# One condition row spread by TensorE, one root for four tiles of x, and slot 0 with high and low weights in turn

## The chip, the core and the metric

The kernel runs on one core of a Trainium2 chip. The core has TensorE (PE: matmuls and transposes, with PEld for its weight loads), VectorE (DVE), ScalarE (ACT), GpSimd (POOL) and SyncE (SP), and 16 DMA engines that all issuing engines share. Each engine works through its own instructions in order; PE's matmuls write PSUM, which DVE and ACT read. The metric is the device time of one launch in microseconds, the median over the runs.

## The reference

A gated MLP layer on x of shape (4, 1024, 512), float32, with a condition per batch element:

```python
scale = cond @ norm_w.T + 1.0                     # (4, 512)
ms = mean(x * x, axis=-1)
h = x * (scale[:, None, :] * rsqrt(ms + 1e-6))
val, gate = split(h @ up_w.T, 2, axis=-1)         # up_w: (4096, 512)
h = val * gelu(gate)                              # 2048 wide
y = act_quant(h) @ weight_quant(down_w).T         # 8-bit tokens, ternary weights
return y + x
```

cond is (4, 128), norm_w (512, 128), down_w (512, 2048).

## The kernel before

The four batch elements are worked one after the other, 1024 tokens each, in two halves of 512. The up projection of a batch element has 16 blocks `j` of 128 value rows and 128 gate rows. Its products are fp16 with a split: each float32 operand is a high part and a low part, and a product is high*high + high*low + low*high. From batch 1 on, a block is one call of `slot`, with seven sub-products in place of eight (line 470). In batch 0, where up_w still has to be read, scaled, transposed and split, the products are the plain ones (line 485), and block 0 of the first half has a function of its own, `plain_first` (line 527). Everything is issued in an order written out by hand (`tc.manual_schedule()`), so the order in the text is the order on every engine's queue.

The change touches the start, up to the first matmuls of block 1. Its steps, in the names of the code:

- `cond_load(0, 1)` brings the first row of cond to all 128 partitions (64 KB) on ACT's queue, then norm_w (`nw`) follows. The other three rows come by `cond_load(1, B)` much later.
- `first_load(n)` brings tiles n and n+1 of x (128 tokens x 512, 512 KB together), `w_load(j)` block j of up_w (two of 256 KB, gate `t=1` and value `t=0`), all on SP's queue.
- `keep_warm(n)` issues n matmuls on zeros (line 752).
- `cond_scale` (line 160) is four dot products on DVE; `cond_largest`, `cond_over` (a transpose on PE, line 185), `cond_range` (four small DVE operations) and `cond_spread` (a matmul, line 201) bring the largest scale, rounded down to a power of two, to all partitions; `cond_undo` and `cond_bring_first` divide by it into `scT`.
- `first_sum(n)` squares tile n and sums (ACT, line 712); `rsqrt_start` takes the root of the sums (one ACT square root at 719, five small DVE operations, 720 to 724), for two tiles at a time; `first_scale` multiplies the tile (ACT 729 or DVE 731); `first_turn` transposes it on PE (line 736) into four banks `ptx`.
- `first_high(0, k)` writes the high part of `XP` from bank k (ACT, line 740), `first_low` the low part (DVE, line 744).
- `w_range`, `w_scale`, `w_turn`, `w_high`, `w_low` find the power-of-two range of a weight block, scale it, transpose it on PE (line 273) and write its high parts (ACT, 286 to 289) and low parts (DVE, 295 to 298). `w_evac` (line 302) copies the transposed block out for later sums.
- `plain_first` has two hooks: `second_part` (turn and split the value of block 0, remaining low parts of x, `w_evac(0)`, and the load of the Gelu table, line 813) and `second_slot` (turn and split block 1). After it comes `plain_half(1, 0)`, whose first matmul reuses the bank that block 0's Gelu (line 532) has to read first.

The bank tags "A", "B", "E" and "po" are PSUM banks; R and H are two large SBUF tiles that many views share.

Of the kernel before, what the change touches and what calls it, by code (L numbers as in the profile page):

```python
# [8 lines left out]
F32 = mybir.dt.float32  # L9
# [4 lines left out]
ALU = mybir.AluOpType  # L14
# [3 lines left out]
P = 128  # L18
# [23 lines left out]
def glu_quant_kernel(  # L42
# [10 lines left out]
    PE, ACT, DVE, POOL, SP = nc.tensor, nc.scalar, nc.vector, nc.gpsimd, nc.sync  # L53
    B, S, D = x.shape
    C = cond.shape[1]
    FF = down_w.shape[1]
    TOK = 512
    HALF = D // 2
    NA = TOK // P
    NK = D // P  # L60
# [6 lines left out]
    sm = ctx.enter_context(tc.tile_pool(name="small", bufs=2))  # L67
# [8 lines left out]
    ones = one.to_broadcast([P, P])  # L76
# [8 lines left out]
    H = cpool.tile([P, NSLOT, 2, TOK], F32, name="H")  # L85
# [10 lines left out]
    for n in range(0, P, 32):  # L96
        c = slice(n, n + 32)
# [18 lines left out]
    XP = R[:, 0, 0:4096].bitcast(F16)  # L116
    XP = XP.rearrange("p (l k t) -> p l k t", l=2, k=NK)
# [20 lines left out]
    def bank(tag, bufs, shape=None, name=None):  # L138
        return psum.tile(shape or [P, TOK], F32, name=name or tag, tag=tag, bufs=bufs)

    def po_bank(name, shape=None):
        return bank("po", 3, shape, name)


    scT = cpool.tile([P, NK, B], F32, name="scT")
    dx = cpool.tile([P, B], F32, name="dx")
    ux = cpool.tile([P, B], F32, name="ux")
    nw = R[:, 1, 0:512].rearrange("p (k c) -> p k c", k=NK)
    cb = R[:, 1, 512:1024].rearrange("p (b c) -> p b c", b=B)
    dots = R[:, 1, 1024 : 1024 + C]  # L150
    junk = R[:, 1, 2048:4096].rearrange("p (n d) -> p n d", d=D)

    def cond_load(b0, b1):

        v = cond[b0:b1].rearrange("b c -> (b c)").partition_broadcast(P)
        ACT.dma_start(out=cb[:, b0:b1].rearrange("p b c -> p (b c)"), in_=v)

    def cond_scale(b):
        for k in range(NK):
            DVE.scalar_tensor_tensor(  # L160
                dots, nw[:, k], 1.0, cb[:, b], ALU.mult, ALU.mult, accum_out=scT[:, k, b : b + 1]
            )

    def cond_scale_rest():
# [23 lines left out]
    def cond_range(pm, b0, b1):  # L188
        n = b1 - b0
        d4 = sm.tile([B, 1], F32, name=f"d4_{b0}", tag="d4")[:n]  # L190
        DVE.tensor_reduce(d4, pm, AX.X, ALU.max)
        DVE.tensor_scalar(d4, d4, 1e-30, None, ALU.max)
        pow2_floor(d4)
        dg = sm.tile([B, B], F32, name=f"dg_{b0}", tag="dg")[:n, :n]
        DVE.tensor_scalar(dg, ident[:n, :n], d4, 1.0 / X_UP, ALU.mult, ALU.mult)
        return dg

    def cond_spread(dg, b0, b1, tag):
        n = b1 - b0
        pd = bank(tag, {"po": 3}.get(tag, 2), [P, B], f"pd_{b0}")[:, :n]  # L200
        PE.matmul(pd, ones[:n, :], dg, start=True, stop=True)
        return pd

    def cond_undo(pd, b0, b1):
        DVE.tensor_copy(dx[:, b0:b1], pd)
        DVE.reciprocal(ux[:, b0:b1], dx[:, b0:b1])
# [35 lines left out]
    def w_load(j, ts=(1, 0)):  # L242
        for t in ts:
            SP.dma_start(out=wn(j)[:, t], in_=up_v[j][:, t])

    def w_range(j, t0=0, t1=2):
        t = slice(t0, t1)
        am = sm.tile([P, 2], F32, name=f"wam_{j}_{t0}", tag="wam")[:, t]
        DVE.tensor_reduce(am, wn(j)[:, t], AX.X, ALU.max, apply_absolute_value=True)
        pow2_floor(am)  # L250
        DVE.tensor_scalar(sw[:, j, t], am, 2.0**-100, 1.0 / W_UP, ALU.max, ALU.mult)
        if j not in iv:
            iv[j] = sm.tile([P, 2], F32, name=f"iv_{j}", tag="iv", bufs=3)
        DVE.reciprocal(iv[j][:, t], sw[:, j, t])
# [4 lines left out]
    def w_scale(j, ts=(1, 0), eng=POOL):  # L259
        for t in ts:  # L260
            w, r = wn(j)[:, t], iv[j][:, t : t + 1]
            if eng is ACT:
                ACT.activation(w, w, AF.Copy, scale=r)
            else:
                eng.tensor_scalar(w, w, r, 1.0, ALU.mult, ALU.mult)
# [25 lines left out]
    def w_low(j, ts=(1, 0)):  # L291
        gate, a21, a22 = a_parts(j)
        g, v = (p.rearrange("p (n f) -> p n f", n=2) for p in pw[j])
        if 1 in ts:
            DVE.tensor_tensor(gate[:, :, 1], g, gate[:, :, 0], ALU.subtract)
        if 0 in ts:
            DVE.tensor_tensor(a21[:, 1], v[:, 0], a21[:, 0], ALU.subtract)
            DVE.tensor_tensor(a22[:, 1], v[:, 1], a22[:, 0], ALU.subtract)
# [216 lines left out]
    def plain_first(between):  # L515

        ps = {1: bank("B", 1, name="pg_0_0"), 0: bank("A", 2, name="pv_0_0")}
        gate, a21, a22 = a_parts(0)
        for n, (t, w, l) in enumerate(
            ((1, 0, 0), (1, 1, 0), (0, 0, 0), (0, 1, 0), (1, 0, 1), (0, 0, 1))  # L520
        ):
            if n in between:
                between[n]()
            a = [gate[:, 0], gate[:, 1]] if t else [a21, a22]
            a = [v.rearrange("p w (k f) -> p w k f", k=2) for v in a]
            for k in range(NK):
                PE.matmul(
                    ps[t], a[k // 2][:, w, k % 2, :], XP[:, l, k, :TOK],
                    start=w + l + k == 0, stop=l == 1 and k == NK - 1,
                )  # L530
        t1 = wpool.tile([P, TOK], F32, name="g_0_0", tag="t1")
        ACT.activation(t1, ps[1], AF.Gelu, scale=gain(0, 1))  # L532
        DVE.scalar_tensor_tensor(h_half(0, 0), ps[0], gain(0, 0), t1, ALU.mult, ALU.mult)
# [156 lines left out]
    start_t = sm.tile([P, 1], F32, name="start_t", bufs=1)  # L690
    eps = sm.tile([P, 1], F32, name="eps", bufs=1)
    DVE.memset(eps, EPS)
    cond_load(0, 1)
    ACT.dma_start(out=nw, in_=norm_w.rearrange("(k p) c -> p k c", p=P))
    ACT.activation(start_t, one, AF.Sqrt)

# [9 lines left out]
    ssq0 = sm.tile([P, 8], F32, name="ssq0", bufs=1)  # L706
    rs0 = sm.tile([P, 8], F32, name="rs0", bufs=1)

    def first_sum(n, eng=ACT):
        v, j, a = X0[:, n], junk[:, n % 4], ssq0[:, n : n + 1]  # L710
        if eng is ACT:
            ACT.activation(j, v, AF.Square, accum_out=a)
        else:
            eng.scalar_tensor_tensor(j, v, 1.0, v, ALU.mult, ALU.mult, accum_out=a)

    def rsqrt_start(t, y):

        z = sm.tile([P, 2], F32, name="newton", tag="newton")
        ACT.activation(z, t, AF.Sqrt, scale=1.0 / D, bias=eps)
        DVE.tensor_scalar(t, t, 1.0 / D, EPS, ALU.mult, ALU.add)  # L720
        DVE.reciprocal(y, z)
        DVE.tensor_tensor(z, y, y, ALU.mult)
        DVE.scalar_tensor_tensor(z, z, -0.5, t, ALU.mult, ALU.mult)
        DVE.scalar_tensor_tensor(y, z, 1.5, y, ALU.add, ALU.mult)

    def first_scale(n, eng):
        r = rs0[:, n : n + 1]
        if eng is ACT:
            ACT.activation(X0[:, n], X0[:, n], AF.Copy, scale=r)
        else:  # L730
            eng.tensor_scalar(X0[:, n], X0[:, n], r, 1.0, ALU.mult, ALU.mult)

    def first_turn(n, pts):
        for k in range(NK):
            c = (n % NA) * P
            PE.transpose(pts[k][:, c : c + P], X0[:, n, k * P : (k + 1) * P], ident)  # L736

    def first_high(h, k, pt):
        c = slice(h * TOK, (h + 1) * TOK)
        ACT.activation(XP[:, 0, k, c], pt, AF.Copy, scale=scT[:, k, 0:1])  # L740
# [7 lines left out]
    def keep_warm(n):  # L748

        pz = bank("A", 2, name="pz")  # L750
        for i in range(n):
            PE.matmul(pz, warm[:, :P], warm, start=True, stop=True)

    first_load(0)
    w_load(0, (1,))
    first_load(2)
    w_load(0, (0,))
    w_load(1)
    first_load(4)
    first_load(6)  # L760
    w_load(2)
    keep_warm(18)
    first_sum(0)
    first_sum(1)
    cond_scale(0)
    mx = cond_largest(0, 1)
    pm = cond_over(mx, 0, 1, "A")
    rsqrt_start(ssq0[:, 0:2], rs0[:, 0:2])
    first_scale(0, ACT)
    first_scale(1, ACT)  # L770
    keep_warm(4)
    pd = cond_spread(cond_range(pm, 0, 1), 0, 1, "A")
    first_sum(2)
    first_sum(3)
    w_range(0, 1, 2)
    w_scale(0, (1,), DVE)
    cond_undo(pd, 0, 1)
    cond_bring_first()
    rsqrt_start(ssq0[:, 2:4], rs0[:, 2:4])
    keep_warm(2)  # L780
    ptx = [po_bank(f"ptx_0_{k}") for k in range(3)] + [bank("A", 2, name="ptx_0_3")]
    first_turn(0, ptx)
    first_turn(1, ptx)
    w_turn(0, [bank("E", 2, name=f"pw_0_{t}") for t in (1, 0)], (1,))
    w_high(0, (1,))
    keep_warm(6)
    first_scale(2, ACT)
    first_scale(3, DVE)
    first_turn(2, ptx)
    first_turn(3, ptx)  # L790
    w_range(0, 0, 1)
    w_scale(0, (0,), DVE)
    w_gain(0)
    first_high(0, 0, ptx[0])
    w_low(0, (1,))
    first_high(0, 1, ptx[1])
    first_high(0, 2, ptx[2])
    first_high(0, 3, ptx[3])
# [1 line left out]
    w_gain(1)  # L800
    w_scale(1, (0,))
    first_low(0, 0, ptx[0])
    cond_load(1, B)

    def second_part():
        w_turn(0, ts=(0,))
# [114 lines left out]
        s_low(j, POOL)  # L921
        s_spill(j)

    plain_first({1: second_part, 4: second_slot})
    w_load(3)
    w_evac(1)
    first_sum(4)
# [45 lines left out]
    dg = cond_range(pm, 1, B)  # L973
# [304 lines left out]
```

## Time and profile before

| | us |
|---|---|
| median of 3 runs | 754.97 (754.72 to 755.78) |
| the profiled execution | 754.75 |
| its span, first to last instruction | 752.9 |
| PE busy | 740.7 |
| DVE busy | 550.0 |
| ACT busy | 376.9 |
| POOL busy | 199.2 |

In the profile, times count from the first instruction of the span. A line such as "9.24 0.29 DVE L160 ..." has start, duration, engine, source line, operation, and what is written from what. A note in brackets gives the idle time of the engine just before and what ended it. PEclk is the clock that TensorE was granted, as a share of full speed. Matmul ends are modelled, so the distance between starts says more of a matmul's cost than its duration. Line numbers are those of the kernel before.

### The profile page before, as it was taken

The numbers are of one execution on the slowest core, as the hardware profiler recorded it, in microseconds if no ns is written. First come the engines' busy times: TensorE is split into PE (matmuls) and PEld (weight loads), VectorE is DVE, ScalarE is ACT, GpSimd is POOL, SyncE is SP. The second block draws the span as 40 slices with busy tenths as digits, with TensorE's granted clock in tenths as the row PEclk, the third lists the DMA queues.
The fourth block names the chain that finished last, engine by engine and source line by source line (L and its number), as shares of the span: only waits on it lengthen the run. The fifth ranks groups of instructions, "written<-read, shape, count | busy, mean of one in ns | idle before, by whom it ended". The sixth has DMA issues, their size and how long they took to land.

```text
span 752.9 us, 9580 instructions
## 1 busy us (share of the span) xinstructions
PE 740.7 (98%) x3476; PEld 345.6 (46%) x3494; DVE 550.0 (73%) x800; ACT 376.9 (50%) x618; POOL 199.2 (26%) x218
## 2 busy tenths in 40 slices
PE   7999999999999999999999999999999999999997
PEld 3554554454444444444444444444444444444443
DVE  5777698988889885455779886444779887445896
ACT  4758555556235655443434657353433666332174
POOL 0389577999110030333010030333020000000200
PEclk9999999999999999999999999999999999999999
DMA  6269558776822434565832415367822333333243
GB/s 227 81 213 276 173 178 207 181 200 182 224 84 99 126 101 144 166 210 141 222 122 98 126 64 179 136 168 202 196 99 97 105 112 110 111 102 111 81 158 112
DMA packets 94360, 111.54 MB, mean 148 GB/s; under 512 B 61413, under 2 KB 62181, under 8 KB 94314
## 3 DMA queue, kind: packets, MB, share of 16 engines
q1 hardware_dynamic: 93498, 110.42, 49.1%
q10 hardware_dynamic: 816, 0.52, 0.3%
q8 instruction: 27, 0.44, 0.2%
q14 instruction: 19, 0.16, 0.1%
HBM read 74.73 MB, written 23.09 MB: 130 GB/s over the span
## 4 chain that ended last, share of the span: by engine, by line
PE 92%; DVE 2%; DMA 2%; ACT 1%; issue 1%; POOL 0%; ACTq 0%; SPq 0%; DVEq 0%; POOLq 0%
PE A L470 32%; PE E L470 16%; PE po L678 11%; PE pg L485 9%; PE pv L485 9%; PE B L470 8%; PE po_end L678 4%; PE pw L273 2%; DMA R<-in_L_cond_norm_w_dram 1%; DMA s_dram<-SXY 1%; DMA SXY<-s_dram 1%; PE ptx L736 1%; ACT R L740 0%; DVE R L744 0%; DVE H L171 0%
## 5 line engine op out<-in xcount | busy, mean ns | idle before, releaser
L470 PEld LDWEIGHTS <-SXY 128*128 128x128 f16 x2016 | 197.1, 98 | 238.4 <-DMA SXY<-s_dram 1.0
L470 PE MATMUL A<-R,SXY 128*128 128x512 f16 x1152 | 264.8, 379 | 0.2 <-DMA SXY<-s_dram 0.2
L470 PE MATMUL E<-R,SXY 128*128 128x512 f16 x576 | 140.0, 379 | 0.0
L564 DVE SCALAR_TENSOR_TENSOR H<-A,sg,t 128x512 f32<-128x512 f32 x48 | 36.0, 750 | 81.1 <-PE A L470 81.1
L575 ACT ACTIVATE t<-t,sg 128x512 f32<-128x512 f32 x48 | 34.6, 720 | 106.5 <-DVE t L574 106.5
L678 PE MATMUL po<-wd,R 128*128 128x512 bf16 x369 | 82.4, 379 | 0.8
L678 PEld LDWEIGHTS <-R 128*128 128x128 bf16 x512 | 50.1, 98 | 60.4
L652 DVE TENSOR_TENSOR H<-H,am 128x1024 f32<-128x1024 f32 x64 | 76.2, 1217 | 0.0
L613 POOL PARTITION_ALL_REDUCE am<-R x8 | 14.6, 1820 | 220.5 <-DVE R L599 220.5
L597 DVE TENSOR_REDUCE gm<-H 128x512 f32<-128x1024 f32 x56 | 69.0, 1232 | 2.9 <-DMA wd<-tn 1.9
L470 PE MATMUL B<-R,SXY 128*128 128x512 f16 x288 | 70.0, 379 | 0.0
L574 DVE TENSOR_TENSOR t<-E,t 128x512 f32<-128x512 f32 x48 | 32.6, 680 | 49.3 <-PE E L470 49.3
L379 POOL TENSOR_TENSOR rs<-ssq,neghalf 128x2 f32<-128x2 f32 (+1 forms) x13 | 9.6, 739 | 205.5 <-DVE ssq L378 205.4
L485 PE MATMUL pv<-R 128*128 128x512 f16 x246 | 61.6, 379 | 0.0
L485 PE MATMUL pg<-R,SXY 128*128 128x512 f16 x252 | 57.8, 379 | 0.2 <-ACT g L532 0.2
L485 PEld LDWEIGHTS <-SXY 128*128 128x128 f16 x378 | 37.0, 98 | 42.7 <-issue 0.5
L485 PEld LDWEIGHTS <-R 128*128 128x128 f16 x366 | 35.8, 98 | 41.8
L561 ACT ACTIVATE t<-B,sg 128x512 f32<-128x512 f32 x48 | 33.0, 688 | 36.9 <-PE B L470 36.9
L660 ACT ACTIVATE H<-H 128x1024 f32<-128x1024 f32 x39 | 40.9, 1049 | 20.8 <-DVE H L652 20.8
L545 ACT COPY t<-A 128x512 f32<-128x512 f32 x48 | 28.1, 585 | 45.3 <-PE A L470 45.0
L556 ACT COPY v<-E 128x512 f32<-128x512 f32 x48 | 28.2, 587 | 32.4 <-PE E L470 28.1
L599 DVE TENSOR_TENSOR R<-R,gm 128x512 f32<-128x512 f32 x56 | 42.0, 750 | 1.4
(152 smaller groups left out, 898.3 us busy)
## 6 DMA issues: line engine op xcount, KB each, us to landing
SXY<-s_dram SPq DMA_DIRECT2D x48, 640.0 KB, 4.0
SXY<-s_dram SPq DMA_DIRECT2D x48, 256.0 KB, 4.4
s_dram<-SXY SPq DMA_DIRECT2D x11, 896.0 KB, 4.8
H<-in_L_cond_up_w_dram SPq DMA_DIRECT2D x32, 256.0 KB, 4.1
xr<-in_x_dram SPq DMA_DIRECT2D x19, 256.0 KB, 4.8
out_dram<-xr SPq DMA_DIRECT2D x19, 256.0 KB, 2.3
s_dram<-R SPq DMA_DIRECT2D x5, 896.0 KB, 11.9
H<-in_x_dram SPq DMA_DIRECT2D x8, 512.0 KB, 6.9
```

The costliest lines, as they stand in the source:

```text
L470: PE.matmul(o, s[:, w, k, :], tv[:, :, c, l, k, :], start=start and n == 0, stop=stop and n == len(TERMS) - 1, skip_group_check=True,)
L485: PE.matmul(ps, a[k // 2][:, w, k % 2, :], XP[:, l, k, h * TOK : (h + 1) * TOK], start=n == 0, stop=n == len(terms) - 1,)
L556: ACT.copy(cur["v"], cur["E"])
L561: ACT.activation(cur["t1"], pb, AF.Gelu, scale=gain(g, 1))
L564: DVE.scalar_tensor_tensor(h_half(g - 1, 0), prev["A"], gain(g - 1, 0), prev["t1"], ALU.mult, ALU.mult)
L574: DVE.tensor_tensor(prev["t2"], prev["E"], prev["t2"], ALU.add)
L575: ACT.activation(prev["t2"], prev["t2"], AF.Gelu, scale=gain(g - 1, 1))
L597: DVE.tensor_reduce(gm[0], v, AX.X, ALU.max, apply_absolute_value=True)
L599: return [largest, lambda: DVE.tensor_tensor(m, m, gm[0], ALU.max)]
L652: DVE.tensor_tensor(v, v, r.to_broadcast([P, 2, TOK]), ALU.mult)
L660: ACT.activation(v, v, AF.Copy, bias=MAGIC)
L678: PE.matmul(po, q[:, h, j, a * P : (a + 1) * P], wd[:, j, :], start=j == 0, stop=j == NJ - 1,)
```

## The change

1. cond is read once, as one row of 512 numbers (2 KB) in one partition, on ACT's queue ahead of norm_w. Two matmuls with a column of ones spread it over the partitions, row 0 into one bank and rows 1 to 3 into another. The four dot products of batch 0 read row 0 from PSUM; ACT copies the other rows to `cb`. Both broadcast loads are gone.
2. Tiles 0 to 3 of x are loaded ahead of up_w's block 0, whose two halves follow. All four tiles are squared in a row and share one root; ACT scales tiles 0, 1 and 2, DVE tile 3. They are transposed in the order 0, 3, 1, 2, with the cond spread after the first two.
3. In `plain_first` the gate's high*high and low*high products go in turn for each k; the value's turn is issued before the last k, and `second_slot` where it was, before the products with x's low part.
4. The warm-up matmuls are 6, 5 and 5 in place of 18, 4, 2 and 6. On ACT the first high part of x now comes right behind the gate's; on DVE the gate's low part comes between the value's range and its scaling.

```diff
-    def cond_load(b0, b1):
-
-        v = cond[b0:b1].rearrange("b c -> (b c)").partition_broadcast(P)
-        ACT.dma_start(out=cb[:, b0:b1].rearrange("p b c -> p (b c)"), in_=v)
-
-    def cond_scale(b):
+    cn = H[0:1, 3, 0, : B * C]
+
+    def cond_spread_rows():
+
+        pc = [bank("B", 1, name="pc_0"), bank("E", 2, name="pc_1")]
+        for n, c in enumerate((slice(0, C), slice(C, B * C))):
+            PE.matmul(pc[n][:, : c.stop - c.start], ones[:1, :], cn[:, c], start=True, stop=True)
+        return pc
+
+    def cond_scale(b, rows):
         for k in range(NK):
             DVE.scalar_tensor_tensor(
-                dots, nw[:, k], 1.0, cb[:, b], ALU.mult, ALU.mult, accum_out=scT[:, k, b : b + 1]
+                dots, nw[:, k], 1.0, rows[:, :C], ALU.mult, ALU.mult, accum_out=scT[:, k, b : b + 1]
             )
...
-        for n, (t, w, l) in enumerate(
-            ((1, 0, 0), (1, 1, 0), (0, 0, 0), (0, 1, 0), (1, 0, 1), (0, 0, 1))
-        ):
+        order = [(1, w, 0, k) for k in range(NK) for w in range(2)]
+        order += [(0, w, 0, k) for w in range(2) for k in range(NK)]
+        order += [(t, 0, 1, k) for t in (1, 0) for k in range(NK)]
+        for n, (t, w, l, k) in enumerate(order):
...
-    cond_load(0, 1)
+    ACT.dma_start(out=cn, in_=cond.rearrange("(o b) c -> o (b c)", o=1))
     ACT.dma_start(out=nw, in_=norm_w.rearrange("(k p) c -> p k c", p=P))
...
-        z = sm.tile([P, 2], F32, name="newton", tag="newton")
+        z = sm.tile([P, NA], F32, name="newton", bufs=1)
...
     first_load(0)
-    w_load(0, (1,))
     first_load(2)
-    w_load(0, (0,))
+    w_load(0)
     w_load(1)
     first_load(4)
     first_load(6)
     w_load(2)
-    keep_warm(18)
-    first_sum(0)
-    first_sum(1)
-    cond_scale(0)
+    keep_warm(6)
+    pc = cond_spread_rows()
+    keep_warm(5)
+    for n in range(NA):
+        first_sum(n)
+    cond_scale(0, pc[0])
     mx = cond_largest(0, 1)
     pm = cond_over(mx, 0, 1, "A")
-    rsqrt_start(ssq0[:, 0:2], rs0[:, 0:2])
-    first_scale(0, ACT)
-    first_scale(1, ACT)
-    keep_warm(4)
-    pd = cond_spread(cond_range(pm, 0, 1), 0, 1, "A")
-    first_sum(2)
-    first_sum(3)
+    rsqrt_start(ssq0[:, 0:NA], rs0[:, 0:NA])
+    ACT.copy(cb[:, 1:].rearrange("p b c -> p (b c)"), pc[1][:, : (B - 1) * C])
+    keep_warm(5)
+    for n in (0, 1, 2):
+        first_scale(n, ACT)
+    first_scale(3, DVE)
+    dg = cond_range(pm, 0, 1)
     w_range(0, 1, 2)
     w_scale(0, (1,), DVE)
+    ptx = [po_bank(f"ptx_0_{k}") for k in range(3)] + [bank("A", 2, name="ptx_0_3")]
+    first_turn(0, ptx)
+    first_turn(3, ptx)
+    pd = cond_spread(dg, 0, 1, "A")
+    first_turn(1, ptx)
+    first_turn(2, ptx)
     cond_undo(pd, 0, 1)
     cond_bring_first()
-    rsqrt_start(ssq0[:, 2:4], rs0[:, 2:4])
-    keep_warm(2)
-    ptx = [po_bank(f"ptx_0_{k}") for k in range(3)] + [bank("A", 2, name="ptx_0_3")]
-    first_turn(0, ptx)
-    first_turn(1, ptx)
     w_turn(0, [bank("E", 2, name=f"pw_0_{t}") for t in (1, 0)], (1,))
     w_high(0, (1,))
-    keep_warm(6)
-    first_scale(2, ACT)
-    first_scale(3, DVE)
-    first_turn(2, ptx)
-    first_turn(3, ptx)
+    first_high(0, 0, ptx[0])
     w_range(0, 0, 1)
+    w_low(0, (1,))
     w_scale(0, (0,), DVE)
     w_gain(0)
-    first_high(0, 0, ptx[0])
-    w_low(0, (1,))
     first_high(0, 1, ptx[1])
...
-    cond_load(1, B)
...
-    plain_first({1: second_part, 4: second_slot})
+    plain_first({6: second_part, 16: second_slot})
```

More of the change, by code (lines that the diff above doesn't have):

```diff
@@ L524, in plain_first @@
             a = [gate[:, 0], gate[:, 1]] if t else [a21, a22]
[L525 to L530, printed above, removed]
+            a = a[k // 2].rearrange("p w (k f) -> p w k f", k=2)
+            PE.matmul(
+                ps[t], a[:, w, k % 2, :], XP[:, l, k, :TOK],
+                start=w + l + k == 0, stop=l == 1 and k == NK - 1,
+            )
         t1 = wpool.tile([P, TOK], F32, name="g_0_0", tag="t1")
```

## The prediction

> **What bounds the kernel now.** I read first the share of busy time and the clock row, then the waits of TensorE behind the start, then the chain of the first 27 us, then the start in order of time and in the clock's own stretches. Share of busy time:
>
> ```profile
> PE 740.7 (98%) x3476; PEld 345.6 (46%) x3494; DVE 550.0 (73%) x800; ACT 376.9 (50%) x618; POOL 199.2 (26%) x218
> ```
>
> TensorE (PE) is the bound of the whole. Its waits from 27.1 us to the end (who waited for whom, total us, times, longest):
>
> ```profile
> PE pd L201 <- DVE dg L195: 0.6, 1, 0.6
> PE A L470 <- DMA SXY<-s_dram: 0.2, 1, 0.2
> PE pg L485 <- ACT g L532: 0.2, 1, 0.2
> ```
>
> Only 1.0 us of waiting in 725 us. So what the change wins or loses by the first matmul of block 1 (L485, 27.03 us) goes through to the end almost whole, if the other engines come along; all edits lie ahead of that point. The chain of waits there (start, us, what):
>
> ```profile
> 1.18 7.96 DMA R<-in_L_cond_norm_w_dram
> ...
> 12.50 0.58 PE pd L201 x2
> 13.08 0.97 PE pz L752 x2
> 14.05 1.71 PE ptx L736 x8
> 15.76 0.45 PE pw L273 x4
> 16.21 1.29 PE pz L752 x6
> 17.51 0.78 PE ptx L736 x5
> 18.31 2.43 ACT R L740 x4
> ...
> 23.87 1.28 ACT L813
> ...
> 26.39 0.60 ACT g L532
> ```
>
> The reader sees: norm_w lands at 9.13, then the cond range, then eight transposes of x, warm-up matmuls, the rest of x, then four ACT copies that make XP's high part (L740). Why the second pair of x tiles is late, in order of time (start, us, engine, line):
>
> ```profile
> 7.62 0.63 ACT L712 ACTIVATE R<-H 128x512 f32<-128x512 f32 x1 [4.46 <-DMA H<-in_x_dram]
> 11.70 1.33 ACT L729 ACTIVATE H<-H,rs 128x512 f32<-128x512 f32 x2 [2.42 <-DVE rs L724]
> 14.29 0.30 ACT L719 ACTIVATE newton<-ssq,eps 128x2 f32<-128x2 f32 x1
> 15.28 0.16 DVE L724 SCALAR_TENSOR_TENSOR rs<-newton,rs 128x2 f32<-128x2 f32 x1
> ```
>
> Its data landed at 10.50 (landing events), but its squares wait on ACT behind the first pair's scaling, its root ends at 15.44, and its transposes run at 17.5. The clock, in stretches of 3.41 us (PE busy, PEld, DVE, ACT, POOL, granted clock, DMA share, GB/s):
>
> ```profile
> 5.42:8.84 3.42, 2.02 (x10) 0.69 (x7) 0.00 (x0) 1.22 (x4) 0.00 (x0) 1.00 1.04 369
> 8.84:12.25 3.41, 1.13 (x5) 0.39 (x5) 2.63 (x19) 0.96 (x4) 0.00 (x0) 1.00 1.05 387
> 12.25:15.66 3.41, 3.16 (x13) 2.68 (x14) 3.06 (x15) 2.31 (x7) 0.00 (x0) 0.50 0.81 301
> 15.66:19.07 3.41, 2.96 (x20) 1.81 (x19) 3.27 (x9) 1.97 (x4) 0.00 (x0) 1.00 0.29 86
> ```
>
> A stretch with PE 33% busy was followed by one at half clock; one with 59% busy was not. At half clock eight transposes took 1.71 us (0.21 each), at full clock about 0.11.
>
> **Loads.** The second x pair now goes ahead of both halves of up_w block 0, and a 64 KB broadcast is replaced by one 2 KB row. Ahead of and with that pair lie 1282 KB instead of 1600; at 385 GB/s that is 0.85 us: it lands at 9.65. Block 0's weights come later (the gate half about 10.4, before 8.87), but their range starts on VectorE (DVE) only after 13: nothing, as long as they land by then. The first pair stays at 7.6 or comes up to 0.3 earlier; nothing follows. On SP's queue the load of x tiles 4 and 5 waited 0.9 us for cond; a shorter row can only shorten that. norm_w, second on ACT's queue, lands at 9.13 or up to 1 us earlier.
>
> **Cond.** Added: two fp32 matmuls from one row (128 and 384 columns), queued on PE behind six warm-up matmuls (done about 4.0). Not in the trace; the nearest rows are L201's pair, 0.58 us at one column, and a 512-column warm-up matmul at half clock, 0.43: between 1.1 and 2.2 us, I take 1.7. They end by 6, and DVE needs them when norm_w lands: nothing. If the row landed after 9, every microsecond would count; the broadcast needed 5.7 us from issue, the row should need less. DVE's four dot products now read PSUM: the like operation takes 0.74 from PSUM (L744) against 0.68 (L714), so 4 x 0.06 = 0.24, and mx moves to at most 11.2; the root is later, so nothing. ACT's copy of the other three rows (384 columns, between 0.38 for 256 and 0.59 for 512) fits between the square root and the root's end, 0.8 us in which ACT waits. The later cond load leaves ACT's queue (0.35 us between two L740 copies; the copies already follow each other at 0.6): nothing.
>
> **One root.** Four squares by 9.65 + 1.36 (the first pair took 7.60 to 8.96) = 11.01; from there to the root's end 1.18 as at 14.26 to 15.44: 12.19, instead of 11.67 for the first pair and 15.44 for the second. ACT scales tiles 0, 1, 2 by 12.9, 13.6, 14.2; DVE tile 3 by 12.7. Four columns instead of two change a 0.16 us operation by nothing I can see.
>
> **PE to the gate's turn.** Removed: 18 + 4 + 2 + 6 warm-up matmuls; added 6 + 5 + 5. The last five follow the cond transpose (about 11): they end by 12.2 at full clock, 13.2 at half; 1.1 of half-clock work ahead of the transposes is a cost only in the second case. Then tiles 0 and 3, the cond spread (0.5), tiles 1 and 2, four transposes of the gate. With the half-clock stretch where the trace has it: 12.95 + 0.86 + 0.86 + 0.5, then the rest mostly at full clock: the gate is turned at 16.75 (before 16.2, but with half of x still to come). ACT's gate copy takes 0.5 of issue, so L740 starts at 17.3 instead of 18.31, and ends at 19.75 instead of 20.74.
>
> **DVE.** It runs without a break, by the starts before: tile 3 0.40, cond range 0.79, gate range 1.27, gate scale 0.41, undo and bring 0.57, value range 1.28. From 12.19 and with the short wait for the spread that is 17.1; then the gate's low part, which waits for ACT's gate copy (17.45), 0.60, value scale 0.41, gain 0.13, range of block 1 1.84, first low part of x 0.69. That is 21.1, where before it was 20.83 and then waited 1.4 for the value's copy; this wait is now gone. Value low 0.67, three low parts 1.98, range of block 2 1.85: the low part of block 1's gate starts at 25.6, before 26.81.
>
> **Slot 0.** The 24 matmuls stay 24. High and low weights in turn put the gate's low products into the gaps between L740's copies (0.58 each, with one 0.22 matmul in them). The added wait: the second matmul needs the low gate from DVE (18.05, the first needs 18.0). Everything of PE is behind it, so a late DVE costs one for one here. The value is turned at 19.6 to 20.05, before 21.0 to 21.6; ACT copies it at 20.1, scales block 1, empties the banks, and loads the Gelu table at 22.3 instead of 23.87; copies of block 1 at 23.75; Gelu of block 0 at 24.75; 0.7 later, at 25.4, block 1's first matmul, instead of 27.03. DVE's low gate is ready at 26.3, and PE wants it 0.86 after 25.4: just in time. The sum is 1.63 us. Behind it, DVE waits 1.8 us at 30.3 and ACT 2.1 at 33.8, so neither takes it back.
>
> **A rule and the trace.** The Trainium skill, TensorE: Matmul & The Clock Gate, Part 1, has the clock drop after at least one idle window of 3.4 us, windows that run free of the kernel. The trace is harsher: 1.13 us of work in 3.41 didn't hold it. In the new order PE rests from about 6.8 to 10.9. By the rule this holds a whole window only for one phase in five, all transposes run at full clock, the gate is turned at 15.6, and DVE sets the end: gain 2.05. By the row, the half clock comes again: 1.63; if it already starts at 8.84 the five warm-ups end at 13.2 and it is 1.3. I take the row. Since the windows run free, both ends stay in the range.
>
> **Rivals.** *The clock stays down.* The six warm-ups ahead of the last turns are gone, and PE waits over a microsecond between the gate's turn and slot 0, then in pairs for L740. If PE's share of 15.66 to 19.07 falls from 87% to about 50%, between the 59% that held and the 33% that didn't, slot 0 runs at half clock. One such window costs about 1.1 (754.4); half clock from 12.25 through 22.5 puts L740 back at 18.3 and block 1 at 27.6, 755.5; through 25.9, 757.2. It decides from two windows in a row; taken at 756.4. Against it: by my times the transposes fill 12.95 to 16.75. *The x pair isn't earlier.* If the engines share otherwise and it lands at 10.4, the root ends at 12.95, half of this hides behind the half clock: gain 1.0, 754.0. The same holds if the table load, and not x, sets ACT's order. *The change doesn't do what it says:* norm_w's landing, not cond's, starts the cond range (DVE L160 waits for it, 6.2 us), so the row wins nothing by itself; that is in the sum.
>
> **Numbers.** The profiled execution took 754.75 (span 752.9, 1.85 around it), 0.22 below the median of 754.97; less 1.63 it would take 753.1, the median 753.3. 0.2% is 1.5 us, about what a measurement of this kernel can tell. The forecast's case, gain 1.3 to 2.2 (its own range 752.7 to 753.8), has 0.65, of which some 0.08 stays under 1.5; the late pair 0.15 (754.0, with 0.02 above 1.5); the clock 0.20, of which 0.03 is one window only and little moved. Faster 0.59, same 0.24, slower 0.17. The range takes 752.4 to 755.8 and leaves out half of the clock's case.
>
> **What would show it.** Right: x tiles 2 and 3 squared by 11.1, one root ending near 12.2, the first L740 near 17.3, the table load near 22.3, block 1's first matmul near 25.4, and no new PE wait behind it. Wrong: a half-clock stretch over slot 0, PE waiting there for the low gate for more than half a microsecond, x landing after 10.2, or a gain at 25 us that a later wait eats.

## The result: 752.13 us, 2.8 us faster

Over six runs of each, the changed kernel takes 752.13 us (751.78 to 752.85), the kernel before 754.94 (754.64 to 756.25). The ratio is 0.9961, with a 95% interval of 0.9948 to 0.9974: 0.39% faster. The forecast was 753.3, with a range of 752.4 to 755.8. The direction was right, the size was not: the gain is 2.8 us in place of 1.65, just past the range's end. The profiled execution took 752.28, with a span of 750.5 where before it was 752.9.

Share of busy time, after:

```profile
PE 741.7 (99%) x3484; PEld 344.9 (46%) x3484; DVE 549.4 (73%) x795; ACT 377.5 (50%) x618; POOL 199.4 (27%) x218
```

TensorE's waits from block 1's first matmul on (24.7 to 750 us; who waited for whom, total us, times, longest):

```profile
PE pd L205 <- DVE dg L199: 0.7, 1, 0.7
PE pg L489 <- ACT g L536: 0.5, 1, 0.5
```

(The second ends at 24.59 itself.) What was won at the start went through to the end: block 1 starts at 24.59 instead of 27.03, 2.44 earlier, and the span is 2.4 shorter. The chain of waits up to there (start, us, what):

```profile
1.29 6.28 DMA R<-in_L_cond_norm_w_dram
...
7.68 0.31 DVE R L164 x2
...
9.53 0.35 PE pm L189
9.88 2.13 PE pz L756 x5
12.02 1.71 PE ptx L740 x8
13.72 0.51 PE pd L205 x2
14.23 1.03 PE ptx L740 x8
15.27 0.45 PE pw L277 x4
...
16.33 0.60 ACT R L744
16.97 1.75 PE pg L531 x6
...
21.43 1.28 ACT L813
...
23.95 0.60 ACT g L536
24.59 2.75 PE pg L489 x12
```

norm_w lands at 7.57 instead of 9.13. Five warm-up matmuls in 2.13 us and eight transposes in 1.71 are at half clock, the next eight transposes in 1.03 mostly at full clock (the clock's record puts the step at 14.22). The record begins at a profile's first step to full clock, and a row reads 1.00 ahead of it: the six warm-ups from 1.43 us start 0.43 apart, the spacing of half clock, though the rows there read 1.00. So the 1.00 in the rows from 3 to 4 us below is no full clock. And x comes far earlier than I had it, in order of time:

```profile
4.27 0.63 ACT L716 ACTIVATE R<-H 128x512 f32<-128x512 f32 x1 [1.03 <-DMA H<-in_x_dram]
6.05 0.63 ACT L716 ACTIVATE R<-H 128x512 f32<-128x512 f32 x1 [0.44 <-DMA H<-in_x_dram]
7.41 0.30 ACT L723 ACTIVATE newton<-ssq,eps 128x4 f32<-128x4 f32 x1
9.28 0.16 DVE L724 TENSOR_SCALAR ssq<-ssq 128x4 f32<-128x4 f32 x1
9.95 0.16 DVE L728 SCALAR_TENSOR_TENSOR rs<-newton,rs 128x4 f32<-128x4 f32 x1
```

The reader sees two things. The pairs are squared from 4.27 and 6.05, where the forecast had 7.6 and 9.65. And the squares are done at 7.4, but their root starts on DVE at 9.28: it stands behind the four dot products, which wait for norm_w. The root isn't what the transposes wait for here: it ends at 10.11, and the chain goes from norm_w over the largest scale and five warm-up matmuls to the first transpose at 12.02.

Where the loads got their time is in one row for each kernel, the stretch from 3 to 4 us (the last two numbers are the share of the DMA engines and GB/s). Before:

```profile
3.00:4.00 1.00, 1.00 (x4) 0.33 (x3) 0.07 (x1) 0.16 (x1) 0.00 (x0) 1.00 0.40 77
```

After:

```profile
3.00:4.00 1.00, 1.00 (x3) 0.15 (x1) 0.07 (x1) 0.23 (x2) 0.00 (x0) 1.00 1.04 389
```

Before, over a megabyte of loads had been issued by then, and the engines were 40% busy. The row was there to be read, and I had worked with the later 385 GB/s alone.

### The profile page after: what moved, and what is told of

Read it like the earlier page. It is cut to its first block, busy times and chain, and to the rows that moved or that the text cites. A ratio compares the mean times of both kernels' runs of the same rounds, so it can differ in the third digit from the quotient of the medians.

```text
span 750.5 us, 9573 instructions
## 1 busy us (share of the span) xinstructions
PE 741.7 (99%) x3484; PEld 344.9 (46%) x3484; DVE 549.4 (73%) x795; ACT 377.5 (50%) x618; POOL 199.4 (27%) x218
## 4 chain that ended last, share of the span: by engine, by line
PE 93%; DVE 2%; ACT 2%; DMA 1%; POOL 1%; issue 1%; ACTq 0%; SPq 0%; DVEq 0%; POOLq 0%
PE A L474 32%; PE E L474 16%; PE po L682 11%; PE pg L489 9%; PE pv L489 9%; PE B L474 8%; PE po_end L682 4%; PE pw L277 2%; DMA R<-in_L_cond_norm_w_dram 1%; DMA SXY<-s_dram 1%; PE ptx L740 1%; DVE R L748 0%; DVE H L175 0%; ACT djk L356 0%; POOL SXY L325 0%
## 5 line engine op out<-in xcount | busy, mean ns | idle before, releaser
L682 PE MATMUL po<-wd,R 128*128 128x512 bf16 x384 | 85.3, 379 | 0.0
L556 ACT COPY B<-A 128x512 f32<-128x512 f32 x48 | 27.4, 571 | 31.2 <-PE A L474 30.2
```

The lines of the kernel that those rows point to most:

```text
L682: PE.matmul(po, q[:, h, j, a * P : (a + 1) * P], wd[:, j, :], start=j == 0, stop=j == NJ - 1,)
```

## Experiments

Two theories. First: the broadcast of cond's row, the first load on ACT's queue, held up all loads behind and beside it, and the row read once is the whole gain. Second: the gain is that of the other parts, as forecast (the order of the loads, one root, slot 0), and the row is worth nothing. All ratios are against the kernel before on the same chip.

**The row alone.** The kernel before, and of the change only part 1:

```diff
-    cond_load(0, 1)
+    ACT.dma_start(out=cn, in_=cond.rearrange("(o b) c -> o (b c)", o=1))
...
-    keep_warm(18)
+    keep_warm(6)
+    pc = cond_spread_rows()
+    keep_warm(7)
...
-    cond_scale(0)
+    cond_scale(0, pc[0])
...
+    ACT.copy(cb[:, 1:].rearrange("p b c -> p (b c)"), pc[1][:, : (B - 1) * C])
...
-    cond_load(1, B)
```

> The kernel before with the cond row alone: one 2 KB row, two matmuls that spread it, loads of x and up_w in the old order, two roots, old slot 0. If the broadcast load held up all loads behind it (first theory), the first x pair lands near 4.3 in place of 7.6 and norm_w near 7.6 in place of 9.1, and the time falls by 0.8 to 1.6 us (753.3 to 754.1). If the early landing came from the new order of the loads (second theory), x lands near 7.6 as before and the time stays within 0.3 us of 754.9.

Measured: 751.60 us, ratio 0.9955 (0.9942 to 0.9967). That is the whole gain of the change, and more than either theory expected of this part. norm_w lands at 6.14, and the first pair is squared from 4.16. The chain now goes through TensorE's own warm-ups, at half clock until 12.0 in this profile, and no longer through norm_w:

```profile
6.17 3.10 PE pz L756 x7
9.27 0.21 PE pm L189
...
24.52 2.75 PE pg L489 x12
```

This run also leaves out the late broadcast of cond's other rows and has fewer warm-ups at the start; the broadcast by itself is tested below.

**All but the row.** The changed kernel with its cond loads as before:

```diff
-    ACT.dma_start(out=cn, in_=cond.rearrange("(o b) c -> o (b c)", o=1))
+    cond_load(0, 1)
...
-    pc = cond_spread_rows()
-    keep_warm(5)
+    keep_warm(10)
...
-    cond_scale(0, pc[0])
+    cond_scale(0)
...
     first_low(0, 0, ptx[0])
+    cond_load(1, B)
```

> The changed kernel with cond's broadcast loads as before (row 0 on all partitions at the start, the rest later), five warm-up matmuls in the place of the two that spread the row. First theory: the second x pair lands at 9.6 to 10.5, the root ends near 12.2, and the gain is what was forecast, 1.3 to 2.0 us against before (753.0 to 753.6). Second theory: x lands at 6 as in the changed kernel, and the time is within 0.3 us of 752.1.

Measured: 754.91 us, ratio 0.9997 (0.9988 to 1.0006): nothing. The loads behaved as the first theory says, and close to the forecast (second pair squared from 9.97, root ended 12.50), but the gain that I had worked out from there didn't come. Its clock, in the stretches of its own 3.41 us steps (PE busy, PEld, DVE, ACT, POOL, clock, DMA share, GB/s):

```profile
7.55:10.96 3.41, 0.00 (x0) 0.00 (x0) 0.90 (x6) 2.33 (x7) 0.00 (x0) 1.00 1.06 389
10.96:14.38 3.42, 2.56 (x8) 1.23 (x9) 3.09 (x15) 2.48 (x6) 0.00 (x0) 0.50 1.00 368
14.38:17.79 3.41, 3.41 (x16) 3.06 (x15) 2.10 (x9) 0.10 (x1) 0.00 (x0) 0.50 0.24 90
```

Two stretches at half clock, 6.8 us, not one. The five warm-ups took 2.13, all sixteen transposes ran at 0.21 each, and the gate was turned at 18.6, where the forecast had 16.75. The chain:

```profile
1.18 8.69 DMA R<-in_L_cond_norm_w_dram
...
11.82 0.37 PE pm L185
12.20 2.13 PE pz L752 x5
14.33 1.71 PE ptx L736 x8
16.04 0.51 PE pd L201 x2
16.55 1.64 PE ptx L736 x8
18.19 0.45 PE pw L273 x4
```

Of these 1.9 us, 1.4 lie ahead of the first transpose (14.33 for 12.95), and not all of that is the clock: norm_w landed at 9.87, where the kernel before has 9.13, and the cond transpose stands at 11.8 in place of about 11.

How much the clock takes is in the runs' mean granted clock, which is listed for every run. A stretch of half clock behind the first step to full lowers it by 0.0023 (half of 3.41 in 753 us). Of the eleven runs nine have 0.995, two such stretches, with a median of 755.04; two have 0.998, one stretch, at 753.79 and 754.12. The kernel before beside them has one stretch in sixteen of 22 runs (0.997 or 0.998, median 754.83) and two in six (0.995, median 756.09). So a stretch goes with 1.1 to 1.3 us. With as many stretches, this kernel is about 1 us faster than the kernel before (0.87 and 1.05); most of its runs have one more, and that takes the gain.

**One more broadcast, and one more load of the same size.** To the changed kernel, ahead of all on ACT's queue, a load that nothing uses; first the broadcast, then 128 different rows:

```diff
+    ACT.dma_start(out=cb[:, 0], in_=cond[0:1].rearrange("b c -> (b c)").partition_broadcast(P))
     ACT.dma_start(out=cn, in_=cond.rearrange("(o b) c -> o (b c)", o=1))
```

```diff
+    ACT.dma_start(out=cb[:, 0], in_=norm_w[0:P])
     ACT.dma_start(out=cn, in_=cond.rearrange("(o b) c -> o (b c)", o=1))
```

> The changed kernel with one more load ahead of all on ACT's queue: row 0 of cond to 128 partitions (64 KB, the same 512 bytes read 128 times), used by nothing. First theory: the second x pair lands at 9 or later instead of 6.0, the time rises by 1 to 2 us (753.1 to 754.1). If the broadcast is harmless (second theory): within 0.3 us of 752.1.

> The changed kernel with one more load ahead of all on ACT's queue, as large as the broadcast and in as many pieces (128 of 512 bytes), but of 128 different rows, used by nothing. If reading the same 512 bytes 128 times is what is slow, x lands within 0.5 us of the changed kernel's 4.3 and 6.0, and the time within 0.5 us of 752.1. If 128 small pieces at the head of the queue are slow in themselves, it is like the extra broadcast.

Measured: 756.44 us with the broadcast, ratio 1.0013 (1.0004 to 1.0022); 753.09 with the rows, ratio 0.9972 (0.9960 to 0.9983). As many bytes in as many pieces at the same place cost 4.3 us in one form and 1.0 in the other, by the medians against the changed kernel's 752.13. The stretch from 3 to 4 us with the broadcast:

```profile
3.00:4.00 1.00, 1.00 (x3) 0.15 (x1) 0.07 (x1) 0.69 (x2) 0.00 (x0) 1.00 0.35 77
```

and with the rows:

```profile
3.00:4.00 1.00, 1.00 (x3) 0.15 (x1) 0.07 (x1) 0.69 (x2) 0.00 (x0) 1.00 1.02 385
```

The load itself, from issue to landing (the last number, us): the broadcast, as long as in the kernel before, and the 128 rows:

```profile
R<-in_cond_dram ACTq DMA_DIRECT2D x1, 64.0 KB, 5.7
R<-in_L_cond_norm_w_dram ACTq DMA_DIRECT2D x1, 64.0 KB, 2.5
```

So it isn't the number of pieces, nor their size, but that all read the same 512 bytes. The two loads also read different tensors, but cond as such isn't slow: in the changed kernel its 2 KB row had landed by 2.02. The 4.3 is over the expected 1 to 2 because norm_w, behind it, landed at 11.85, later than in any other kernel here, and the chain starts with norm_w (7.57 in the changed kernel, 4.28 earlier):

```profile
1.74 10.11 DMA R<-in_L_cond_norm_w_dram
```

With the rows, x was squared from 4.42 and 6.06, as expected of the first case, but the time missed it: 1.0 slower, not within half a microsecond. norm_w's landing fits most of that as well: 8.39 against 7.57.

**The broadcast behind norm_w.** The kernel before, with two lines exchanged:

```diff
-    cond_load(0, 1)
     ACT.dma_start(out=nw, in_=norm_w.rearrange("(k p) c -> p k c", p=P))
+    cond_load(0, 1)
```

> The kernel before with its first broadcast of cond issued behind norm_w on ACT's queue instead of ahead of it; all else the same. If the broadcast is harmful by standing at the head of the queue, the engines fill at once (above 300 GB/s from 3 to 4 us, before 77), x lands near 4.5 and norm_w near 6.5, but cond last, and the time falls by 0.5 to 2 us. If it is harmful wherever it stands, x lands near 7 again and the time is within 0.4 us of before or slower.

Measured: 752.42 us, ratio 0.9968 (0.9956 to 0.9981), 2.6 us for an exchange of two lines, a little over what was expected. The first pair is squared from 4.92, norm_w is in at 5.4, and cond comes last, at 7.81:

```profile
1.25 6.57 DMA R<-in_cond_dram
```

From 3 to 4 us the engines move 284 GB/s, a little under the expected 300. The broadcast is slow here too, and holds others: from 6 to 7 us they move only 113 GB/s, and the second x pair lands at 9.19 instead of 8.12 with the row. But nothing on the path waits for that pair. This run says how much of the row's 3.4 us is the broadcast at the head of the queue: 2.6. The intervals of the two overlap, so the other 0.8 is not shown.

**The rest of the change on top of the row.** Two runs add one part each to the row alone. The order of loads:

```diff
     first_load(0)
-    w_load(0, (1,))
     first_load(2)
-    w_load(0, (0,))
+    w_load(0)
```

> The kernel before with the cond row, and of the rest of the change only the order of loads: the second x pair ahead of up_w's block 0. In the changed kernel norm_w landed at 7.57, with the row alone at 6.14. If the earlier x pair delays norm_w and the dot products start the chain, this is 0.5 to 1.2 us slower than the row alone (752.1 to 752.8), with norm_w near 7.5. If the second x pair sets the end, it is 0.5 us or more faster (751.1 or less).

And slot 0, with the loop of the changed kernel:

```diff
-    plain_first({1: second_part, 4: second_slot})
+    plain_first({6: second_part, 16: second_slot})
```

> The kernel before with the cond row, and of the rest of the change only slot 0 with high and low weights in turn. If the Gelu table load and the copies ahead of it on ACT set the end of slot 0, in either order: within 0.3 us of the row alone (751.6). If the turn fills gaps on the path: 0.4 to 0.8 us faster. If the value turned later costs: up to 0.5 us slower.

Measured: the order of loads 752.52 us, ratio 0.9968 (0.9957 to 0.9978); slot 0 in turn 751.33, ratio 0.9944 (0.9932 to 0.9957). The first is slower than the row alone as the first case had it, by 0.9, and norm_w lands at 7.50 as expected, 1.4 later. That the one causes the other is not shown: in the profile of the row alone the chain went through the warm-ups and not through norm_w, and the profiled run with the new order starts block 1 at 24.13, earlier than the 24.52 there. The second is within 0.3 of the row alone, as its first case had it. Both intervals overlap that of the row alone (0.9942 to 0.9967), so each by itself is a direction, not a proof. The one root was not run by itself.

**The root and the warm-ups of the changed kernel.** Without the last warm-ups:

```diff
-    keep_warm(5)
     for n in (0, 1, 2):
         first_scale(n, ACT)
```

> The changed kernel without the last five warm-up matmuls (between the cond transpose and the first transpose of x). If these hold the path (at half clock they take 9.7 to 12.0 us, while the first tile is scaled by 10.85), the transposes start about 0.9 earlier and the time falls by 0.4 to 0.9 us (751.2 to 751.7). If they only cover a wait, or the clock needs them, nothing or up to 1 us slower, with the half clock lasting beyond 14.2 us.

And with the root ahead of the dot products, and the cond range behind the x tiles on PE:

```diff
-    cond_scale(0, pc[0])
-    mx = cond_largest(0, 1)
-    pm = cond_over(mx, 0, 1, "A")
     rsqrt_start(ssq0[:, 0:NA], rs0[:, 0:NA])
...
-    keep_warm(5)
...
     first_scale(3, DVE)
-    dg = cond_range(pm, 0, 1)
+    cond_scale(0, pc[0])
+    mx = cond_largest(0, 1)
     w_range(0, 1, 2)
...
-    first_turn(0, ptx)
     first_turn(3, ptx)
-    pd = cond_spread(dg, 0, 1, "A")
+    first_turn(0, ptx)
     first_turn(1, ptx)
     first_turn(2, ptx)
+    pm = cond_over(mx, 0, 1, "A")
+    keep_warm(2)
+    dg = cond_range(pm, 0, 1)
+    pd = cond_spread(dg, 0, 1, "A")
```

> The changed kernel with the root's operations on DVE ahead of the four dot products, the x tiles turned at once, and the cond transpose, range and spread behind the four turns with two warm-up matmuls in place of five. In the changed kernel the root starts at 9.3, behind the dot products that wait for norm_w (7.57), though the squares are done at 7.4. If that order costs the time that the early x won, the root ends near 8.6, the gate is turned near 14.5 instead of 15.7, and the time falls by 0.6 to 1.2 us (750.9 to 751.5). If DVE's own work sets the end whatever its order, within 0.3 us of 752.1.

Neither was faster: 752.93 us, ratio 0.9968 (0.9955 to 0.9980), and 753.21, ratio 0.9974 (0.9965 to 0.9983), where the changed kernel has 0.9961 (0.9948 to 0.9974). The first fits its second case, the half clock beyond 14.2; the second fits neither of its cases. Without the warm-ups the transposes did start early (10.7 instead of 11.8), but in its profile the clock was halved from 8.06 to 14.88, nearly all of the sixteen transposes were at half clock (1.97 and 1.87 us for eight), and block 1 starts at 24.35, only 0.24 earlier than in the changed kernel. With the root first, it ended at 8.6 as expected, but then the sixteen transposes ran at half clock, and later slot 0 did:

```profile
7.67:11.08 3.41, 1.93 (x9) 1.93 (x10) 3.04 (x17) 2.34 (x5) 0.00 (x0) 0.50 1.06 393
11.08:14.49 3.41, 2.98 (x13) 1.72 (x11) 1.93 (x9) 0.00 (x0) 0.00 (x0) 0.50 0.49 181
14.49:17.91 3.42, 1.92 (x10) 1.10 (x11) 2.85 (x11) 2.43 (x5) 0.00 (x0) 1.00 0.21 77
17.91:21.32 3.41, 3.41 (x12) 1.73 (x10) 2.94 (x8) 1.81 (x5) 0.69 (x1) 0.50 0.08 29
```

After a stretch with PE 56% busy, 17.91 to 21.32 is at half clock, in the middle of slot 0. This is the rival that the forecast feared, in a kernel that had taken work off PE ahead of slot 0. Block 1 starts at 25.44 there.

**Fewer warm-ups with the row alone, and a version meant to be fastest.**

```diff
-    keep_warm(7)
+    keep_warm(3)
```

> The kernel before with the cond row alone, and three warm-up matmuls instead of seven behind the spread. There the largest scale was ready at 7.9 and its transpose waited for warm-ups until 9.3. If that is on the path, the time falls by 0.4 to 1.0 us against the row alone (750.6 to 751.2). If the second x pair (squared at 9.9, scaled at 14.2) sets the end, it stays within 0.3 us of 751.6.

```diff
-    pc = cond_spread_rows()
+    pc0 = cond_spread_rows(slice(0, C), "B", 1)
...
-    keep_warm(4)
+    pc1 = cond_spread_rows(slice(C, B * C), "E", 2)
...
     rsqrt_start(ssq0[:, 2:4], rs0[:, 2:4])
+    ACT.copy(cb[:, 1:].rearrange("p b c -> p (b c)"), pc1)
```

> A version meant to be the fastest: the kernel before with the cond row and slot 0 in turn, but only row 0 is spread at the start, and the matmul for rows 1 to 3 stands where four warm-up matmuls stood, its copy behind the second square root. If the one-row matmuls count little as work for the clock (in the changed kernel PE was busy without a break from 1.4 to 8.4 and stayed at half clock to 14.2), full clock comes earlier in most runs and the time is 0.4 to 1 us under the row with slot 0 in turn (750.3 to 750.9). If they count like others, it stays within 0.3 us of 751.3.

Measured: three warm-ups 752.56 us (751.08 to 753.00), ratio 0.9967 (0.9955 to 0.9979); the split version 751.58 (750.07 to 751.79), ratio 0.9948 (0.9936 to 0.9961). Neither beats what it was built on (751.60 and 751.33): the first fits neither of its cases, the second its second case. The runs of each lie 1.7 to 1.9 apart, and the profiled one is the shortest both times. For three warm-ups it has full clock from 10.15, and block 1 at 23.06, 1.5 before the row alone. So the shorter chain is there, and the other runs give it back. For the split version the mean granted clock says where: it is 1.000 at 750.07 and 750.31, and 0.997 or 0.998, about one half-clock stretch, at 751.58 to 751.79. For three warm-ups it is 0.999 or 1.000 in five of six, but half clock ahead of the first step to full isn't in that number, so there the cause stays open. The fastest of all by median is slot 0 in turn on the row alone, 751.33; its interval (0.9932 to 0.9957) still overlaps the changed kernel's.

**The changed kernel again.**

> The changed kernel again, beside the others on the same chip: 751.8 to 752.9 as before. Its profile shows whether the half clock lasts to 14.2 us again or moves from run to run; if it moves by more than 1 us, so should block 1's first matmul by some tenths.

Measured: 751.75 us, ratio 0.9961 (0.9949 to 0.9974), as the first time. Its profile has another clock: full from 4.63 to 8.05, then half to 14.87, and the step at 14.22 had become one at 14.87. norm_w landed at 7.99 in place of 7.57. Block 1 starts at 25.11, half a microsecond later than in the first profile. So two executions of one kernel differ by half a microsecond in these first 25 us.

## Why the prediction was wrong

- **The step that failed: "the row wins nothing by itself".** The load's cost was put at its 64 KB by the later 385 GB/s, 0.17 us, although the same prediction notes that it "needed 5.7 us from issue", and the first x pair was to stay "at 7.6" or come "up to 0.3 earlier". It came at 4.25, the second pair at 6.03 (forecast 9.65), norm_w at 7.57 (forecast 8.1 to 9.13). The row alone is worth 3.4 us, and all the rest without it 0.0. One more broadcast puts 4.3 us back, so the cause is shown from both sides.
- **The order of loads and the one root: mis-sized the other way.** With the broadcast in place, which is what I had summed, the second pair and the root came where the forecast had them (9.9 and 12.50, for 9.65 and 12.19), but the gain was 0 in place of 1.63. Two terms failed. The half clock was given one stretch and some tenths; nine of eleven runs have two, and a stretch goes with 1.1 to 1.3 us. And norm_w was put at "9.13 or up to 1 us earlier"; behind the earlier second pair it landed at 9.87, and the chain starts with it. With as many half-clock stretches, about 1 us of the 1.63 is there. That the total is only 1.2 off, and on the right side, is luck: two errors of opposite sign.
- **A wait that I had on the wrong side.** "mx moves to at most 11.2; the root is later, so nothing": with the loads early it is the other way round. The squares are done at 7.4 and the root ends at 10.11, since DVE takes the dot products first. But neither sets the transposes, which wait for the largest scale and the warm-ups until 12.02. The early second pair wins little, and with it norm_w comes 1.4 us later (7.57 against 6.14 with the row alone). Moving the root ahead won no time; in its profile the clock took it.
- **Slot 0 held.** From the first L740 (after: L744) to block 1 the forecast had 8.1 us, measured 8.37; DVE's wait of 1.4 for the value's copy is gone; block 1's low gate was written from 24.48, and TensorE did not wait for it.
- **The carry held.** 2.44 us at block 1, 2.4 in the span, no new wait behind it.
- **The skill's rule and the trace's row.** The Trainium skill's page TensorE: Matmul & The Clock Gate, Part 1, asks for an idle window of 3.4 us. I took the trace's row, 33% busy and yet dropped, and the runs bear that out, up to 56%, and up to 68% where the one-row matmuls of the spread are among the work. Its other statement, that the windows run free of the kernel, weighed more than I gave it: the first step to full clock lies between 4.1 and 15.5 us in the profiles here, at 14.22 and 4.63 in the two of the changed kernel.

## What to carry to other kernels

Look at how fast the DMA engines fill before costing a load by its bytes: a row of 77 GB/s with a megabyte outstanding says that something at the head of a queue holds the rest. A broadcast that reads one short row for every partition does not belong ahead of the loads that start the chain; read the row once and spread it, or at least issue it behind them. And where the clock's windows run free, the gain of a shorter start is only as sure as TensorE's work in the 3.4 us before.

## What the runs showed of the hardware

- 128 pieces that read the same 512 bytes took 5.7 us from issue to landing, 128 pieces of different rows 2.5, and the x loads on SP's queue, on the same 16 engines, waited with them (77 against 385 GB/s). Why the same address is slow was not tried further.
- The two matmuls that spread the row (contraction over one row, 128 and 384 columns) took 2.07 us at half clock, and may count for less than other work for the clock. In the profile of the row alone PE was busy without a break from 1.44 us, and the clock stayed at half to 12.0. Without these two, the stretch from 5.17 to 8.59 has 71% of work and didn't release it; in the run with slot 0 in turn, 78% from 1.35 to 4.76 did.
- What held full clock, in stretches without these two, was 59% of work (before, 5.42 to 8.84) and 61% (the broadcast behind norm_w, 5.32 to 8.73); 33% and 56% did not. Stretches with them don't fit into that, counted fully or not at all:

| stretch at full clock | PE busy | without the spread's two | the next stretch |
|---|---|---|---|
| changed kernel again, 4.63 to 8.05 | 59% | 35% | half clock |
| root first, 4.25 to 7.67 | 65% | 35% | half clock |
| one more broadcast, 4.82 to 8.24 | 68% | 35% | half clock |
| slot 0 in turn, 4.76 to 8.17 | 73% | 50% | full clock |

How much a one-row matmul counts stays open. It was not tested by itself: the version that moved the larger of the two away from the start gained nothing.
- Transposes can release the clock: without the last warm-ups, TensorE was busy with them for 2.97 of the 3.41 us from 11.47 to 14.88, and full clock came behind it.
